# Order of the two kinds of scores within each half of a score phase

## Chip, cores and metric

The kernel runs on one core of one Trainium2 chip. The metric is the device time of one execution in microseconds (us); the time given is the median of several runs. TensorE (PE) does the matmuls; its weight loads are shown as an engine of their own (PEld). VectorE (DVE), ScalarE (ACT) and GpSimd (POOL) work beside it, and each engine takes its instructions in the order in which the program lists them.

## What is computed

A block of two layers over x (4 batches of 512 tokens, 256 features). Each layer is a gated cross attention with 16 heads of 16 features over a context, followed by a gated feed-forward part: in layer 0 with weights quantised to -1, 0 and 1, in layer 1 with one of four experts for each token. Attention is the part that matters here (layer 0; layer 1 has no bias in the softmax, and a relu on q, k and v):

```python
scores = jnp.einsum('bhqd,bhkd->bhqk', Q, K) / math.sqrt(D_K)
time_bias = -0.1 * jnp.abs(t[None, :] - t[:, None])
attn = jax.nn.softmax(scores + time_bias[None, None], axis=-1)
out = jnp.einsum('bhqk,bhkd->bhqd', attn, V)
```

## The kernel before

**Two kinds of scores.** Heads are worked on in 32 groups of four (`groups`, L396: 2 layers x 4 batches x 4), and a head of a group lives in 32 of the 128 partitions. The scores of a group are made twice. First *for the maxima*: `maxima` (L505) multiplies q by k for one tile of 128 queries and two heads into two PSUM tiles `pm`, and VectorE reduces each to its row maximum (L517, `m<-pm`). Once all four query tiles have their maxima, `turned` (L568) transposes them on TensorE (`pmT`, L576) and VectorE subtracts them from q (L578), which gives a shifted query `q2`. Then *shifted*: `weights` (L521) multiplies k by `q2` for one tile of 128 keys and two heads into two PSUM tiles `psc`, and ScalarE takes the exponential of each (L532, `p<-psc`); in layer 0 GpSimd multiplies the block on the diagonal by a decay (L535). Each of these matmuls uses 32 rows of TensorE's array (the program gives pair 0 the first two of the four row groups and pair 1 the last two). `weighted` (L553) multiplies the exponentials of a whole group by the values (`po`, L560).

**Units and score phases.** There are 128 units (32 groups x 4 tiles), and `scores(u, vs)` (L540) is the score phase of unit u: its shifted scores, and, six units ahead, the maxima of unit u + 6. It has two halves. The first holds pair 0 of the maxima and pair 1 of the shifted scores, the second pair 1 of the maxima and pair 0 of the shifted scores. In each half all four matmuls are listed first, and the two functions' drains (two reductions, two exponentials) after them. So a unit fills eight PSUM tiles, in the order pm pm psc psc, pm pm psc psc. Before unit 0 there are only maxima, and in the last six units only shifted scores; units 0 and 1 have two units' maxima each.

**PSUM places.** Every product of TensorE goes to a tile of one pool, `ps` (L55): eight tiles under one tag, each a whole bank. They are given out in turn, so each new tile takes the place of the one eight tiles before it, and its first matmul waits until that one has been read for the last time: by VectorE's reduction if it was a `pm`, by ScalarE's exponential if it was a `psc`, by whatever reads it otherwise.

**Slots.** Behind the score phase of a unit `slot(u)` (L977) lists other work: every fourth unit `weighted`; two units later `turned`, which also transposes and divides the group before (`pn`, L583); and, up to a planned cost of about 3.1 us, steps of chains written out with costs and due times: key and query projections (`pk`, `pq`, L460), values (`pva`, L429), transposes of normalised rows (`pt`, L380), layer 0's feed-forward (`ph`, L640; `py_f`, L388), the output projection (`py_wo`, L388), routing (`plT`, `plg`, `prk`). A slot takes one to four PSUM tiles, which VectorE and ScalarE read. A step of the chains that costs TensorE nothing is the normalisation of a batch's rows: four ACTIVATE instructions on ScalarE (L365, `xn<-x,off,rstd`).

**Stages.** About 40 us of loads and first projections, the units from about 40 to 705 us, and then the experts of layer 1, with gathers and scatters by indirect DMA.

Of the kernel before, what the change touches and what calls it, by code (L numbers as in the profile page):

```python
# [44 lines left out]
def flamingo_kernel(ctx: ExitStack, tc: tile.TileContext, t: dict, out: bass.AP):  # L45
# [494 lines left out]
    def scores(u, vs):  # L540

        ms = [(maxima, v, pair) for v in vs for pair in range(2)]
        ws = [(weights, u, 1 - pair) for pair in range(2)] if 0 <= u < n_units else []
        while ms or ws:
            if ms and ws:
                quad = [ms.pop(0), ws.pop(0)]
            else:
                left = ms or ws
                quad = [left.pop(0), left.pop(0)]
            for drain in [f(w, pair) for f, w, pair in quad]:  # L550
                drain()
# [478 lines left out]
    for u in range(-NT, n_units):  # L1030
        if u == -NT + 1:
            key_rows(0, 1, nc.vector)
            other_half()
            early_none()
            early()
        if u == -NT + 2:
            totals1()
            early_rows()
            totals2()
        if u == 0:  # L1040
            turned(0, None)
            other_constants()
        if u == 4:
            maxima_places(1)
        if u == first_unit(0, B - 1) + 1:
            attn_w.append(load_attn(1))
        if u == first_unit(1, 2) + 2:

            wo1 = [const.tile([P, NF // 2, D], F32, tag=f"cT{i}", name=f"wo1{i}") for i in range(2)]
            for i, w in enumerate(wo1):  # L1050
                rw = t["wo1"][i * FF // 2 : (i + 1) * FF // 2, :]
                nc.sync.dma_start(out=w, in_=rw.rearrange("(c p) f -> p c f", p=P))
        if u == n_units - 1:
            turn_tile(0)
        vs = [u + NT] if u < 0 else [2 * u + NT, 2 * u + NT + 1] if u < LEAD - NT else [u + LEAD]
        scores(u, [v for v in vs if v < n_units])
        slot(u)
# [179 lines left out]
```

## Time and profile before

| what | value |
|---|---|
| median of 3 runs (lowest to highest) | 873.18 us (870.64 to 873.26) |
| the profiled execution's own time | 873.53 us |
| span of the profiled execution | 871.8 us |
| mean granted clock of TensorE | 0.982 |
| TensorE busy from 40 to 700 us | 651.75 of 660 us |
| VectorE, ScalarE busy from 40 to 700 us | 440.8 and 348.9 us |
| reductions `m<-pm` (L517) | 512, mean 682 ns |
| exponentials `p<-psc` (L532) | 512, mean 602 ns |
| score matmuls (L503) | 1024 records for `pm`, 1024 for `psc` |

A row of the timeline gives the start in us from the span's start, the length (of the whole group when instructions are merged), engine, line, operation, the tiles as out<-in, the shapes, and how many (x4); in brackets the time the engine sat idle before it and what ended that. TensorE works a 32-bit matmul off in two passes, so each stands as two records. Matmul ends are modelled, so starts are the surer numbers.

### The profile page before, as it was taken

The numbers are of one execution on the slowest core, as the hardware profiler recorded it, in microseconds if no ns is written. First come the engines' busy times: TensorE is split into PE (matmuls) and PEld (weight loads), VectorE is DVE, ScalarE is ACT, GpSimd is POOL, SyncE is SP. The second block draws the span as 40 slices with busy tenths as digits, with TensorE's granted clock in tenths as the row PEclk, the third lists the DMA queues.
The fourth block names the chain that finished last, engine by engine and source line by source line (L and its number), as shares of the span: only waits on it lengthen the run. The fifth ranks groups of instructions, "written<-read, shape, count | busy, mean of one in ns | idle before, by whom it ended". The sixth has DMA issues, their size and how long they took to land. (4 is left out here: it accounts for less than half of the span.)

```text
span 871.8 us, 13667 instructions
## 1 busy us (share of the span) xinstructions
PE 840.1 (96%) x5290; PEld 476.7 (55%) x5290; DVE 539.9 (62%) x1167; ACT 427.7 (49%) x902; POOL 270.0 (31%) x430
## 2 busy tenths in 40 slices
PE   6899999999999999999999999999999999999995
PEld 3444444445464455545446444554444458999994
DVE  6677878556746675567663776567677715644443
ACT  2765555553645563546543664346565463233331
POOL 5336456324233343312100220012002034445542
PEclk9899999999999999999999999999998899999998
DMA  9100000000001000000000010001001046556650
GB/s 316 55 1 1 1 1 1 1 1 1 2 6 32 1 1 1 1 25 1 1 1 1 25 49 1 1 1 49 2 1 48 2 146 211 155 184 200 198 191 15
DMA packets 17776, 42.03 MB, mean 48 GB/s; under 512 B 2158, under 2 KB 12144, under 8 KB 15280
## 3 DMA queue, kind: packets, MB, share of 16 engines
q0 software_dynamic: 5168, 27.08, 9.5%
q1 hardware_dynamic: 12128, 13.54, 4.6%
q8 instruction: 42, 0.69, 0.3%
q10 hardware_dynamic: 416, 0.54, 0.2%
q14 instruction: 22, 0.18, 0.1%
HBM read 34.86 MB, written 6.68 MB: 48 GB/s over the span
## 5 line engine op out<-in xcount | busy, mean ns | idle before, releaser
L517 DVE TENSOR_REDUCE m<-pm 128x1 f32<-128x512 f32 x512 | 316.9, 682 | 136.3 <-PE psc L503 128.1
L532 ACT ACTIVATE p<-psc 128x512 f32<-128x512 f32 x512 | 267.4, 602 | 161.5 <-PE psc L503 157.2
L503 PE MATMUL psc<-q,k 32*128 32x512 f32 x1024 | 286.4, 636 | 2.1 <-DVE m L517 1.9
L503 PE MATMUL pm<-k,q 32*128 32x512 f32 x1024 | 269.6, 625 | 2.9 <-DVE m L517 2.0
L535 POOL TENSOR_TENSOR p<-p,dec 128x256 f32<-128x256 f32 x128 | 93.5, 734 | 184.0 <-ACT p L532 184.0
L503 PEld LDWEIGHTS pm<-k,q 32*128 32x128 f32 x1024 | 96.7, 186 | 87.6 <-issue 59.9
L503 PEld LDWEIGHTS psc<-q,k 32*128 32x128 f32 x1024 | 108.5, 186 | 55.2 <-issue 26.2
L560 PE MATMUL po<-p,v 128*32 128x512 f32 x1024 | 119.8, 609 | 1.7 <-DVE m L517 1.6
L1075 ACT ACTIVATE ha<-pg,wg 128x128 f32<-128x128 f32 x152 | 43.2, 368 | 88.7 <-PE pg L1069 88.7
L560 PEld LDWEIGHTS po<-p,v 128*32 128x32 f32 x1024 | 32.1, 112 | 85.6 <-issue 64.5
L1069 PE MATMUL pg<-xs,wg 128*128 128x128 f32 x608 | 71.3, 276 | 1.0 <-DVE xn_f L369 1.0
L1069 PEld LDWEIGHTS pg<-xs,wg 128*128 128x128 f32 x608 | 70.4, 192 | 3.0 <-POOL rstd_f L347 1.3
L1085 PE MATMUL pyf<-wo,ha 128*128 128x256 f32 x304 | 68.6, 380 | 0.0
L599 POOL TENSOR_TENSOR x<-x,o 128x256 f32<-128x256 f32 x14 | 10.2, 729 | 174.6 <-DVE o L592 142.7
L640 PE MATMUL ph<-xTf,w1q 128*128 128x512 f32 x128 | 60.2, 603 | 0.0
L1085 PEld LDWEIGHTS pyf<-wo,ha 128*128 128x128 f32 x304 | 56.4, 190 | 6.8
L566 ACT COPY oT<-po 128x512 f32<-128x512 f32 x32 | 18.7, 585 | 84.4 <-PE po L560 84.4
L388 PE MATMUL py_f<-w2q,h 128*128 128x256 f32 x256 | 57.0, 381 | 0.0
L388 PEld LDWEIGHTS py_f<-w2q,h 128*128 128x128 f32 x256 | 48.1, 190 | 9.2 <-DVE m L517 3.0
L1089 DVE TENSOR_TENSOR y<-y,pyf 128x256 f32<-128x256 f32 x19 | 8.0, 421 | 53.3 <-PE pyf L1085 53.0
L460 PE MATMUL pk<-cT,wk 128*128 128x512 f32 x64 | 33.0, 641 | 7.4 <-DMA cT<-in_ctxT_dram 7.3
L640 PEld LDWEIGHTS ph<-xTf,w1q 128*128 128x128 f32 x128 | 22.4, 190 | 27.7 <-issue 17.2
(203 smaller groups left out, 801.6 us busy)
## 6 DMA issues: line engine op xcount, KB each, us to landing
x<-in_x_dram SPq DMA_DIRECT2D x4, 512.0 KB, 8.7
rows_d<-xn_f SPq DMA_DIRECT2D x4, 512.0 KB, 3.7
rows_d<-x SPq DMA_DIRECT2D x4, 512.0 KB, 3.9
cT<-in_ctxT_dram SPq DMA_DIRECT2D x3, 512.0 KB, 9.5
w1q<-in_w_dram SPq DMA_DIRECT2D x1, 1024.0 KB, 9.4
w2q<-in_w_dram SPq DMA_DIRECT2D x1, 1024.0 KB, 11.6
wo<-in_wo_dram SPq DMA_DIRECT2D x2, 512.0 KB, 3.7
rows<-in_rows_dram SPq DMA_DIRECT2D x1, 640.0 KB, 9.6
```

Source lines behind the costliest of these rows:

```text
L388: nc.tensor.matmul(py[:, n, :], lhsT=operand(c, n0 + n), rhs=w[:, c, :], start=(c == 0), stop=(c == chunks - 1),)
L460: nc.tensor.matmul(pp, lhsT=attn_w[layer][w][:, c, ts(tt, P)], rhs=src[:, c, :], start=(c == 0), stop=(c == NC - 1),)
L503: nc.tensor.matmul(out_, lhsT=lhs[r, ts(n, P)], rhs=rhs[r, :], start=True, stop=True)
L517: nc.vector.tensor_reduce(m[:, n, 2 * pair + i, r : r + 1], pm[i], AX.X, ALU.max)
L532: nc.scalar.activation(p[:, i, :], psc[i], AF.Exp, scale=SCALE)
L535: nc.gpsimd.tensor_tensor(d, d, dec.unsqueeze(1).to_broadcast([P, 2, P]), ALU.mult)
L560: nc.tensor.matmul(po[i * HP : (i + 1) * HP, :], lhsT=v_sb[b % 2][0][:, kt, c0 : c0 + HP], rhs=ps_exp[NT * s + kt, i // 2][:, i % 2, :], s ...
L566: nc.scalar.copy(pos[s], po)
L640: nc.tensor.matmul(ph, lhsT=w1q[:, c, ts(f, P)], rhs=st["xT"][:, c, :], start=(c == 0), stop=(c == NC - 1),)
L1069: nc.tensor.matmul(ph[:, f, :], lhsT=w[:, c, ts(f2 * NF // 2 + f, P)], rhs=xs[j][:, c, :], start=(c == 0), stop=(c == NC - 1),)
L1075: nc.scalar.activation(ha[:, f, :], ph[:, f, :], AF.Gelu, bias=wg[j][:, NC * FF + fa : NC * FF + fa + 1],)
L1085: nc.tensor.matmul(py, lhsT=hs[j, f // 4][:, f % 4, :], rhs=wo1[f // 4][:, f % 4, :], start=(f == 0), stop=(f == NF - 1),)
```

## The change

In `scores`, where a half has both kinds, the shifted scores are taken first and the maxima second. A unit's eight PSUM tiles then come in the order psc psc pm pm, psc psc pm pm. The pairs that meet in a half stay the same; so do the halves that hold only one kind. In each half the exponentials are now listed ahead of the reductions, which stand on another engine.

```diff
@@ -543,7 +543,7 @@
         ws = [(weights, u, 1 - pair) for pair in range(2)] if 0 <= u < n_units else []
         while ms or ws:
             if ms and ws:
-                quad = [ms.pop(0), ws.pop(0)]
+                quad = [ws.pop(0), ms.pop(0)]
             else:
                 left = ms or ws
                 quad = [left.pop(0), left.pop(0)]
```

## Prediction

> **What bounds the kernel now.** First the page's busy shares and the row of TensorE in 40 slices.
>
> ```profile
> PE 840.1 (96%) x5290; PEld 476.7 (55%) x5290; DVE 539.9 (62%) x1167; ACT 427.7 (49%) x902; POOL 270.0 (31%) x430
> PE   6899999999999999999999999999999999999995
> ```
>
> TensorE is full from about 40 to 700 us, where the 128 score phases ("units") lie; a unit and the slot work behind it take some 5 us. Whatever makes TensorE wait there is time. So I read one undisturbed unit in the timeline, engine by engine. It starts at 288.28; the first fence is TensorE, the second the first instruction of each draining engine and the first weight load of the slot work behind the unit.
>
> ```profile
> 288.28 0.70 PE L503 MATMUL pm<-k,q 32*128 32x512 f32 x2
> 288.29 0.70 PE L503 MATMUL psc<-q,k 32*128 32x512 f32 x2
> ...
> 289.67 0.59 PE L503 MATMUL psc<-q,k 32*128 32x512 f32 x2
> 289.68 0.59 PE L503 MATMUL pm<-k,q 32*128 32x512 f32 x2
> 290.20 3.70 PE L640 MATMUL ph<-xTf,w1q 128*128 128x512 f32 x8
> ```
> ```profile
> 289.44 0.69 DVE L517 TENSOR_REDUCE m<-pm 128x1 f32<-128x512 f32 x1 [3.08 <-PE psc L503]
> 289.58 0.60 ACT L532 ACTIVATE p<-psc 128x512 f32<-128x512 f32 x1 [0.59 <-PE psc L503]
> 290.20 0.19 PEld L640 LDWEIGHTS ph<-xTf,w1q 128*128 128x128 f32 x1 [0.76 <-DVE m L517]
> ```
>
> The four matmuls of a half start within 0.02 us: they run side by side in four row groups, so their order in the half is worth 0.01 us by itself. The unit's last matmul starts at 289.68 and slot work follows 0.52 us later, 1.93 us after the unit began. I find that 0.52 in every undisturbed unit: TensorE's own pace. The row names a reduce as what ended the loader's wait, and rightly: the slot's first PSUM place is the unit's first place (eight places, used in turn), and its reduce ended at 289.44 + 0.69 = 290.13, only 0.07 before. It costs nothing today, but has next to no slack.
>
> **What the change does.** In the built program each mixed half now issues psc, psc, pm, pm; nothing is added or removed, and VectorE, ScalarE and GpSimd keep their own order, as do SP's queue and all DMAs. What changes is who frees a place eight places on. A slot's first two places wait for the unit's first two exps instead of its first two reduces, the third and fourth for reduces instead of exps. After a slot of two places, the next unit's places 3 and 4 wait for exps 3 and 4 instead of reduces 3 and 4, and reduces 3 and 4 are wanted half a phase later.
>
> **Part 1, clean units: +0.6 us.** First exp: 289.58 + 0.60 = 290.18, 0.05 behind the first reduce, and two places earlier in the half it ends 0.01 sooner. A matmul that a drain releases starts 0.05 behind its end in the trace (many score matmuls do), so the slot starts at about +1.94 for +1.93: 0.01 x some 30 units = 0.3. Slots that open with `po` in layer 0 wait for two semaphores and follow 0.11 behind; nine of these x 0.04 = 0.3.
>
> [...]
>
> **Part 2, units whose exps are late: the main term.** ScalarE is a queue in order, and the four normalisation rows of L365 (28 + 28 instructions, 14 groups of four) stand ahead of a unit's exps. At 402.47:
>
> ```profile
> 403.09 2.07 ACT L365 ACTIVATE xn_a<-x,off_a,rstd_a 128x256 f32<-128x256 f32 x4
> 405.06 2.03 ACT L532 ACTIVATE p<-psc 128x512 f32<-128x512 f32 x4
> ```
> ```profile
> 404.40 0.19 PEld L388 LDWEIGHTS py_wo<-wo,oTT 128*128 128x128 f32 x1 [0.76 <-DVE m L517]
> ```
>
> The exps wait until 405.06; the first ends at 405.64 (two take 1.06, one 0.58). Today nobody cares: the slot opens at 404.40 on the place that a reduce freed. Afterwards it opens at 405.64 + 0.05 = 405.69, and TensorE stands for 1.29 us. I looked at every group of L365 inside the score stage: 13 units (starts 128.09, 155.24, 220.68, 255.90, 309.83, 361.58, 402.47, 476.47: 1.27 to 1.30 us each; 497.33, 590.41, 667.39: 1.23; 507.29, 599.37: 0.55, where the slot is late already). Gross: 8 x 1.28 + 3 x 1.23 + 2 x 0.55 = 15.0.
>
> Some comes back, because the next unit already waits for something that the late exps or the slot's drains cause, and that does not move as much. Unit 159.51, behind 155.24, runs 1.17 over the clean 1.93: about 1.1 back. 481.19, behind 476.47, runs 0.40 over: 0.4 back. Behind 590.41 and 667.39 the next unit is held today by the late exps (0.84 over); reckoned place by place it ends 0.28 later instead of 1.23: 1.9 back for both. At 497.33 the slot is a transpose of those same rows, whose second half runs at +2.91 today and could at +3.72: 0.8 paid, 0.4 back. The others are followed by units with 0 to 0.07 over, or by a drain chain that moves along: nothing back. Net: 15.0 - 3.9 = **+11.1**.
>
> **Part 3, slots that a late reduce holds today: -2.4.** At 102.50 VectorE has a quantising step between reduces:
>
> ```profile
> 106.06 1.16 DVE L295 SCALAR_TENSOR_TENSOR w1q<-w1q,qthr_w,neg_w 128x512 f32<-128x512 f32 x1
> 107.14 0.68 DVE L517 TENSOR_REDUCE m<-pm 128x1 f32<-128x512 f32 x1
> ```
> ```profile
> 107.96 1.50 PE L560 MATMUL po<-p,v 128*32 128x512 f32 x12 [0.64 <-DVE m L517]
> ```
>
> That idle 0.64 goes, since the exps are long done. The same kind of gap: 0.49 at 89.69, 0.52 at 586.84, 0.47 at 120.81, 0.21 at 139.80 and 0.11 at 680.42 (last score matmul + 0.52 against the slot's start). What is late next there is VectorE's own backlog: in the stretches 78 to 110 and 113 to 126 it has hardly a gap, so I count only the place where such a stretch ends and leave out two more (0.7 each) inside one.
>
> **Part 4, reduces wanted half a phase later: -1.4.** Units behind a two-place slot stop waiting at place 4 for reduce 4: 0.26 at 375.67, 0.4 at 121.83, 0.15 at 677.71, 0.6 at 689.97. Others are held by the last places of the unit, which wait for the slot's own drains; these keep their place (1.39 instead of 0.97 into the unit, some 15 units) and stay. Bounds: 0, if exp 4 is as late, to 4.5, the sum of today's waits at place 4.
>
> **Part 5, turned slots: -1.0.** `pn` behind `pmT` starts at +2.50, 0.05 behind reduce 2; exp 2 ends 0.06 sooner: 0.07 x 10 + 0.04 x 6.
>
> **Sum.** 0.6 + 11.1 - 2.4 - 1.4 - 1.0 = **+6.9 us**. The profiled execution took 873.5 us (span 871.8); the median of the runs is 873.2, so the difference is the same against either: **880.4 us**.
>
> **Rivals.**
> 1. *Faster.* Reduces, not exps, are the slow drain: VectorE is 62% busy against 49%, and the waits view has more than ten lines in which a matmul or load waits for the reduce. If the late exps are handed back by later waits everywhere, as behind 155.24 (part 2 falls to 2), and parts 3 to 5 reach their upper bounds (2.4 + 1.4, 4.5, 1.0), the sum is 0.6 + 2 - 9.3 = -6.7: 867 us. It decides once more than about three quarters of the 15.0 comes back. Against it: by the rows of part 2, eight of the 13 units hand nothing back.
> 2. *No change.* Part 2 at about 5 (some six of its 11.1 handed back as well, by more successors like 159.51): 0.6 + 5 - 4.8 = +0.8: 874 us.
> 3. *More.* Nothing is handed back and VectorE's backlog eats parts 3 and 4: 0.6 + 15.0 - 1.0 = +14.6: 888 us.
> That the program keeps its order is excluded by its listing.
>
> **How the numbers follow.** Forecast 0.70 (876 to 885), rival 1 0.08, rival 2 0.13, rival 3 0.09. A run can tell 0.3% (2.6 us) from no change, so slower 0.79, same 0.13, faster 0.08. The range reaches over rival 2's centre and most of rival 3: 874 to 887.
>
> **What would show it.** Right: in the 13 units the slot's first load is released by the exp (ACT p L532), TensorE stands about 1.2 us there, and the waits view gets 10 to 15 us of TensorE or its loader behind ACT p; DVE's lines for `po`, `pk`, `ph` and `pmT` shrink; the gap at about 107.9 is gone; clean units still take 1.93 to 1.95. Wrong: clean units grow by more than 0.05 (part 1 mis-sized, 100 units), or no unit waits for an exp, or the rows of L365 come at another time than before.

## The result, and the profile after

| | before | changed | changed / before |
|---|---|---|---|
| median of the runs compared (lowest to highest) | 873.12 us (870.64 to 873.26, 4 runs) | 885.89 us (885.43 to 886.52, 4 runs) | 1.0155, 95% interval 1.0143 to 1.0166 |
| span of the profiled execution | 871.8 us | 884.4 us | |
| mean granted clock there | 0.982 | 0.982 | |

Slower by 12.8 us where 7.2 was forecast (880.4: the sum of 6.9 on top of the profiled 873.5). First the page of the changed kernel: busy shares, TensorE's slices, and the row of the granted clock.

```profile
PE 842.2 (95%) x5290; PEld 481.5 (54%) x5290; DVE 539.2 (61%) x1167; ACT 426.3 (48%) x902; POOL 270.6 (31%) x430
PE   6899999999999999999999999999999999999995
PEclk9999999999999999999999999999998789999998
```

The same work in a longer span. Only the clock row has something to ask about: ahead of the last slices it has an 8, a 7 and an 8, where the kernel before has two eights.

The clean unit that started at 288.28 now starts at 289.67; timeline of the changed kernel, its first and last score matmul, its drains, and the first weight load of its slot:

```profile
289.67 0.70 PE L503 MATMUL psc<-q,k 32*128 32x512 f32 x2
...
290.89 1.57 ACT L532 ACTIVATE p<-psc 128x512 f32<-128x512 f32 x3 [0.51 <-PE pm L503]
290.91 1.89 DVE L517 TENSOR_REDUCE m<-pm 128x1 f32<-128x512 f32 x3 [3.05 <-PE pm L503]
...
291.60 0.30 PEld L640 LDWEIGHTS ph<-xTf,w1q 128*128 128x128 f32 x2 [0.76 <-ACT p L532]
```

The slot follows 1.93 us after the unit's start, as before, but the loader's releaser is now the exponential. The exponentials also start earlier: 1.22 into the unit, where it was 1.30.

The unit that started at 402.47 now starts at 406.27 (timeline, ScalarE, VectorE and the loader):

```profile
406.89 2.07 ACT L365 ACTIVATE xn_a<-x,off_a,rstd_a 128x256 f32<-128x256 f32 x4
...
407.51 2.48 DVE L517 TENSOR_REDUCE m<-pm 128x1 f32<-128x512 f32 x4 [3.05 <-PE pm L503]
...
408.86 1.54 ACT L532 ACTIVATE p<-psc 128x512 f32<-128x512 f32 x3
409.49 0.51 PEld L388 LDWEIGHTS py_wo<-wo,oTT 128*128 128x128 f32 x3 [2.06 <-ACT p L532]
```

The slot opens 3.22 us into the unit instead of 1.93. The first reduction is over at about 408.2, but nobody waits for it; the first exponential, behind the four rows of L365, ends 0.05 before the load. In the waits view (total, times, longest, in us) of the changed kernel:

```profile
PEld pmT L576 <- ACT p L532: 20.2, 25, 2.0
PEld pk L460 <- ACT p L532: 10.6, 13, 2.1
PEld py_wo L388 <- ACT p L532: 8.2, 4, 2.1
PE py_wo L388 <- ACT p L532: 4.9, 4, 1.2
```

The loader's rows are not loss as they stand: a clean unit has 0.76 in them. What the longest (2.1) have beyond that, and TensorE's own row (four times 1.2 at `py_wo`), is.

**Where the time went, unit by unit.** I took the start of each score phase and of the slot behind it in both traces and noted where the changed kernel's lag grows or shrinks (places are starts in the kernel before):

| place | part of the prediction | predicted | measured |
|---|---|---|---|
| clean units, 1.93 in both | 1 | +0.6 | 0.0 |
| the 13 units with late exps: eight by 1.27 to 1.30, three by 1.23 or 1.24, two by 0.55 | 2, gross | +15.0 | +15.1 |
| units behind five of them (159.51, 481.19, 502.49, 593.85, 670.84) | 2, handed back | -3.9 | -3.2 |
| slots that a late reduce held (77.28, 102.50, 117.57, 137.63, 580.74, 677.71; nothing at 83.84, whose slot is the 89.69 of the prediction) | 3 | -2.4 | -2.5 |
| place 4 (121.83, 375.67, 684.54) | 4 | -1.4 | -1.1 |
| 15 slots, 13 of them turned, 0.10 to 0.16 each | 5 | -1.0 | -1.8 |
| 204.26, 298.64, 412.01, 528.23: 0.22 each | none | 0 | +0.9 |
| 324.97, 367.14, 417.72, 451.25, 544.89, 623.78, 635.55: 0.08 to 0.24 | none | 0 | +1.2 |
| first units, 31 to 42 (clock) | none | 0 | -0.8 |
| the rest, singly up to 0.5, both signs | none | 0 | +0.4 |
| **lag where the units with maxima end (694)** | | **+6.9** | **+8.2** |
| end of the score stage, 694 to 709 | none | 0 | +3.8 |
| behind it | none | 0 | +0.6 |
| **span** | | **+6.9** | **+12.6** |

Up to 694 us the sum holds within 1.3. Beyond it comes a term that the prediction does not have. The windows view at that place (span of the window, busy us of each engine, and behind POOL the mean granted clock, the DMA share and GB/s), the kernel before, then the changed one:

```profile
693.00:700.00 7.00, 7.00 (x48) 4.74 (x46) 3.76 (x14) 2.34 (x5) 0.73 (x1) 0.74 0.01 2
700.00:707.00 7.00, 7.00 (x52) 2.06 (x48) 0.04 (x1) 2.86 (x6) 5.40 (x6) 0.76 0.63 197
707.00:714.00 7.00, 6.96 (x49) 4.87 (x42) 1.25 (x4) 6.98 (x13) 1.60 (x2) 1.00 0.66 258
```
```profile
700.00:707.00 7.00, 7.00 (x28) 4.42 (x28) 4.63 (x12) 2.66 (x5) 0.73 (x1) 0.50 0.01 2
707.00:714.00 7.00, 7.00 (x34) 3.96 (x38) 0.75 (x5) 1.95 (x4) 2.72 (x3) 0.50 0.13 42
714.00:721.00 7.00, 6.80 (x49) 2.62 (x42) 0.88 (x4) 2.99 (x7) 3.55 (x4) 0.90 0.90 334
```

By the clock records the changed kernel runs at half clock from 698.4 to 715.5 (17.1 us), the kernel before from 689.7 to 696.6 and from 700.0 to 703.4 (10.2). TensorE is all but full there (6.80 to 7.00 of 7 us in the rows above) and the clock is 0.50, so by an estimate from these two about half of the 6.9 us more is lost, 3.4 of the 3.8. The largest piece is the small matmuls of L860, 24 records that took 2.87 us at full clock before and 5.29 at half clock now (timeline, the kernel before and the changed one):

```profile
696.49 2.87 PE L860 MATMUL pid_d<-tid_d,sel_d 128*128 128x9 f32 x24
```
```profile
704.66 5.29 PE L860 MATMUL pid_d<-tid_d,sel_d 128*128 128x9 f32 x24
```

### The profile page after: what moved, and what is told of

It reads as the page before. It is cut to its first block, busy times and chain, and to the rows that moved or that the text cites. A ratio compares the mean times of both kernels' runs of the same rounds, so it can differ in the third digit from the quotient of the medians.

```text
span 884.4 us, 13653 instructions
## 1 busy us (share of the span) xinstructions
PE 842.2 (95%) x5290; PEld 481.5 (54%) x5290; DVE 539.2 (61%) x1167; ACT 426.3 (48%) x902; POOL 270.6 (31%) x430
## 4 chain that ended last, share of the span: by engine, by line
PE 76%; issue 6%; ACT 5%; DVE 4%; DMA 4%; POOL 4%; POOLq 0%; ACTq 0%; DVEq 0%
PE psc L503 15%; PE pm L503 14%; PE po L560 13%; PE py_f L388 6%; PE ph L640 6%; PE pk L460 4%; PE pva L429 3%; PE pq L460 3%; DMA out_dram<-y,put 2%; PE pmT L576 2%; PE py_wo L388 2%; PE pg L1069 2%; DVE m L517 2%; PE pn L583 1%; ACT xn_f L365 1%
## 5 line engine op out<-in xcount | busy, mean ns | idle before, releaser
L532 ACT ACTIVATE p<-psc 128x512 f32<-128x512 f32 x512 | 264.5, 603 | 155.4 <-PE pm L503 137.3
L503 PE MATMUL pm<-k,q 32*128 32x512 f32 x1024 | 286.1, 628 | 1.6 <-ACT q L492 0.9
L503 PE MATMUL psc<-q,k 32*128 32x512 f32 x1024 | 269.4, 627 | 2.4 <-DVE m L517 1.5
L503 PEld LDWEIGHTS pm<-k,q 32*128 32x128 f32 x1024 | 111.5, 185 | 57.2 <-issue 25.7
L503 PEld LDWEIGHTS psc<-q,k 32*128 32x128 f32 x1024 | 95.1, 187 | 83.3 <-issue 48.8
L599 POOL TENSOR_TENSOR x<-x,o 128x256 f32<-128x256 f32 x14 | 10.2, 731 | 179.9 <-DVE o L592 146.7
## 6 DMA issues: line engine op xcount, KB each, us to landing
w2q<-in_w_dram SPq DMA_DIRECT2D x1, 1024.0 KB, 11.5
```

The lines of the kernel that those rows point to most:

```text
L503: nc.tensor.matmul(out_, lhsT=lhs[r, ts(n, P)], rhs=rhs[r, :], start=True, stop=True)
L532: nc.scalar.activation(p[:, i, :], psc[i], AF.Exp, scale=SCALE)
```

## Experiments

No kernel here leaves out or changes any of the computation; they only order it differently. Where an edit is one condition, it stands in the line that the change touches:

```diff
-                quad = [ws.pop(0), ms.pop(0)]
+                quad = [ws.pop(0), ms.pop(0)] if COND else [ms.pop(0), ws.pop(0)]
```

**The 13 units left in the old order** (COND: `u not in (21, 26, 37, 43, 53, 61, 69, 81, 85, 87, 101, 103, 117)`).

> The swapped order everywhere but in the 13 units whose first exponential stands behind the normalisation rows (units 21, 26, 37, 43, 53, 61, 69, 81, 85, 87, 101, 103, 117); those keep the order of before. Theory A (those 13 slots carry the loss): up to the last mixed unit the kernel is 3 to 4 us ahead of before; with the last 15 us of the score stage at half clock as in the changed kernel (+3.8) it ends at 873 to 874 us, without that at 869 to 870. Rival B (the loss is spread over all slots, a little each): only a tenth of it goes, 884 us.

Measured 866.75 us (865.93 to 871.0, 7 runs) against 872.93 of the kernel before: ratio 0.9949, 0.9931 to 0.9967. The loss is gone and a gain is left, larger than theory A said. At the old 402.47, timeline of this kernel, ScalarE and the loader:

```profile
400.10 2.07 ACT L365 ACTIVATE xn_a<-x,off_a,rstd_a 128x256 f32<-128x256 f32 x4
...
401.41 0.94 PEld L388 LDWEIGHTS py_wo<-wo,oTT 128*128 128x128 f32 x5 [0.76 <-DVE m L517]
...
402.08 0.58 ACT L532 ACTIVATE p<-psc 128x512 f32<-128x512 f32 x1
```

The slot opens 0.67 us ahead of the exponential, on a reduction's place. Up to 653 us the lag is -3.0, of which -0.5 came about in the first units, where the clock differs; at 708 it is -7.8. Between 650 and 720 us this trace has 6.8 us of half clock and the kernel before 17.1, so most of the surprise is clock (below).

**The new order in those 13 units alone** (COND: `u in` the same list).

> The order of before, swapped in those 13 units alone. Theory A: the lag up to the last mixed unit is about +12 us, and the end of the score stage keeps the clock of before: 884 to 886 us. Rival B: 874 to 875 us. Rival C (the longer half clock at the end follows from any shift of the stage, not from the order of the last mixed unit): 888 to 889 us.

Measured 883.62 us (882.96 to 884.48, 4 runs), ratio 1.0132, 1.0117 to 1.0146: 0.4 under theory A's range and far from the rivals. Its lag at 653 us is +11.8, where theory A said about +12; the two rows of part 2 in the table above come to 11.5 up to there.

**The new order everywhere but in unit 121, and in unit 121 alone** (COND: `u != 121`; `u == 121`). Unit 121 is the last one with both kinds of scores; it starts at 684.54, just ahead of the half clock.

> The swapped order everywhere but in unit 121, the last one that has maxima. Theory A (with the half clock at the end set off by that unit's order): 3.8 us of the end come back and 0.6 of that unit is lost: 882 to 883 us. Rival C: the long half clock stays, 886 to 887 us.

> The order of before, swapped in unit 121 alone. Theory A: 0.6 us gained in that unit, then 17 us at half clock instead of 10: 876 us. Rival C: the clock of before, 872.5 us.

Measured 883.31 us (882.64 to 883.8, 4 runs; 1.0123, 1.0108 to 1.0137) and 869.29 us (868.08 to 876.1, 12 runs; 0.9973, 0.9957 to 0.9989). My theory that the order in unit 121 sets off the longer half clock falls both ways: kept, the 17.1 us of half clock stay (from 696.9); alone, the kernel gets faster. The first time is near theory A's 882 to 883, but not by its cause: this trace has no half clock between 659 and 675, where the kernel before and the changed one have 6.8 us each. The second lies below both forecasts, and holds a lesson. Up to unit 121 its order is that of the kernel before, and still this is the windows view at 659 us, the kernel before and then this one:

```profile
652.00:659.00 7.00, 5.97 (x39) 3.20 (x35) 6.72 (x16) 4.21 (x8) 0.00 (x0) 1.00 0.00 0
659.00:666.00 7.00, 7.00 (x33) 2.09 (x33) 4.09 (x10) 2.28 (x4) 2.44 (x8) 0.51 0.00 0
```
```profile
652.00:659.00 7.00, 5.97 (x36) 3.36 (x37) 6.69 (x18) 4.15 (x8) 0.00 (x0) 1.00 0.00 0
659.00:666.00 7.00, 6.48 (x57) 2.04 (x50) 3.97 (x9) 3.28 (x8) 2.44 (x8) 1.00 0.00 0
```

The same work, the same stand of TensorE ahead of it (1.03 us in both), once followed by 6.8 us of half clock and once not: 2.4 us of lag that the order cannot have made. Its 12 runs spread over 8 us, and the longer ones have the lower clock: 866.4 us of span at a mean clock of 0.989, 871.0 at 0.982, 874.4 at 0.978.

**The new order in the first half of each unit alone, and in the second half alone** (COND: `len(ws) == 2`; `len(ws) == 1`).

> The new order in the first half of a unit alone; the second half as before. The slot behind a unit opens on the places of the first half. Theory A (the loss is the slot's first two places waiting for exps that stand behind the rows of L365): the whole loss of the 13 units stays, some +11.5 to +12 in the score stage, the gains at slots that a late reduce held stay too, the gain at place 4 (1.4) is lost: 884 to 888 us. Theory B (what counts is which drain holds the last places of a unit): nothing of the loss is left, 870 to 875.

> The new order in the second half of a unit alone. The slot's first two places are freed by reduces again. Theory A: no unit waits for a late exp at its slot, the 13 units lose nothing; place 4 waits for an exp instead of a reduce (-1.4, less where exps are late, as behind the 13 units): 870 to 874 us. Theory B: most of the loss stays, 880 or more.

Measured 882.65 us (878.66 to 883.88, 4 runs; 1.0105, 1.0086 to 1.0125) and 873.28 us (871.5 to 874.75, 12 runs; 0.9995, 0.9985 to 1.0005). The loss sits in the first half, whose places the slot takes: all 13 stands are there at 1.23 to 1.30 or 0.55, and the median is 1.3 under theory A's range. The two longer runs (883.88) have a mean clock like that of the kernel before (0.983), the two shorter ones a higher one (0.987 and 0.991). The second half by itself is worth nothing that can be told: it gains 0.26 at 375.67 and 0.58 at 684.54 and gives 0.38 back at 593.85 and at 670.84, behind late exps.

**The rows out of the way of the exps.** The step `norm` (L365) is kept back until the next unit's scores are listed, and the transposes that need its rows come one unit later (in all three chains that have them; one is shown); once with the new order, once with the old:

```diff
-            [(stats, 0, 0), (more_stats, 0, 1), (norm, 0, 1), (turn, 0.9, 1)],
+            [(stats, 0, 0), (more_stats, 0, 1), (norm, 0, 1), (turn, 0.9, 2)],
...
-            job()
+            pending.append(job) if job.__name__ == "norm" else job()
...
         scores(u, [v for v in vs if v < n_units])
+        while pending:
+            pending.pop(0)()
```

> The changed kernel with the four normalisation rows of L365 issued behind the next unit's scores, so that ScalarE has the unit's exps ahead of the rows; the transposes that need the rows come one unit later. To be read against the next kernel, which has the same rows with the order of the kernel before. Theory A (the loss comes from exps behind the rows): with no late exp left only the gains remain, so this kernel is 3 to 7 us faster than the next one. Theory B (a place freed by an exp is worse by itself, wherever the rows stand): it is 8 to 12 us slower than the next one.

> The kernel before with the rows of L365 issued behind the next unit's scores, as in the kernel ahead. Both theories: within 4 us of the kernel before (869 to 877), since there the slots open on reduces; it is the measure for the kernel ahead.

Measured 869.89 us with the new order (867.95 to 872.31, 8 runs) and 876.92 with the old (875.98 to 879.15, 6 runs): 7.0 us faster, at the upper end of theory A. The move by itself costs: with the old order it is 3.6 us slower than the kernel before (1.0054, 1.0037 to 1.007), with the new one 3.4 faster (0.9969, 0.9953 to 0.9986). Between the two, the same change that costs 12.8 us gains 7.0 once the exps stand ahead of the rows; by the traces the lag between the two is 0.0 at 42 us and -6.6 at 652, so this is not clock. Timeline of the first of the two at the old 402.47:

```profile
400.74 2.06 ACT L532 ACTIVATE p<-psc 128x512 f32<-128x512 f32 x4 [0.43 <-PE pm L503]
...
401.51 3.10 PEld L388 LDWEIGHTS py_wo<-wo,oTT 128*128 128x128 f32 x15 [0.76 <-ACT p L532]
...
402.66 2.08 ACT L365 ACTIVATE xn_a<-x,off_a,rstd_a 128x256 f32<-128x256 f32 x4
```

The slot still opens on an exponential's place, 1.93 us into the unit.

**The idle stretch ahead of the half clock.** In unit 121 TensorE waits for reductions that stand behind 17 small steps of the token lists (L773 to L827) on VectorE. First these steps were moved behind the reductions, in the changed kernel and in the one that keeps the 13 units:

```diff
-            job()
+            if u == 120 and job.__name__ in ("lists", "token_places", "by_tile"):
+                pending.append(job)
+            else:
+                job()
```

> The changed kernel with the 17 small VectorE steps of the token lists (L773 to L827 of the changed kernel) moved from ahead of the reduces of unit 121 to behind them; nothing else. The changed kernel's TensorE idles for 1.46 us in that unit, waiting for a reduce behind these steps, and the 17.1 us of half clock begin in the next clock window. Theory A (the idle stretch sets off the half clock): no half clock between 690 and 720, about 17.1 x 0.44 = 7.5 less and 1.5 less for the idle stretch, up to 2.5 back for the later lists: 876 to 880 us, mean clock 0.988 or more. Theory B (the half clock comes by itself, or from the small matmuls of L860): 10 us or more of half clock stay near 700, 884 to 887 us.

> The new order in all units but the 13 with late exps, and the small VectorE steps behind the reduces of unit 121. Theory A (both costs are apart from one another): the 866.7 of the 13 kept units, less 6.8 x 0.44 = 3 of half clock and up to 1.5 of idle, plus up to 2.5: 862 to 866 us. Theory B (the half clock stays): 866 to 869.

Measured 882.85 us (882.28 to 883.86, 4 runs; 1.0101, 1.0084 to 1.0118) and 866.41 us (866.1 to 870.29, 6 runs; 0.9928, 0.991 to 0.9947). The first lies between the ranges, with 10.2 us of half clock from 703.2, which is what theory B said of the clock; the second lies in theory B's range, 0.3 us below the kernel without the move. But the edit did not do what theory A needs: the stand was not taken away; it moved, and the half clock with it. So the matmuls of L860 were moved as well, one slot later, behind `po`:

```diff
+                if u == 123 and "gathered" in c["steps"][0][0][0].__qualname__:
+                    continue
```

> The changed kernel with the 17 small VectorE steps behind the reduces of unit 121 and the matmuls of L860, which wait for them, one slot later, behind unit 124 and its weighted values: TensorE has other work in both places where it idled. Theory A (the half clock at the end of the score stage follows an idle stretch of TensorE): no half clock between 690 and 725, 17.1 us x 0.4 = 7 less, and 1.5 of idle: 876 to 879 us. Theory B (the half clock comes by itself or from the matmuls of L860): 10 us or more of half clock stay there, 882 to 886 us.

> The same two moves on the kernel that keeps the old order in the 13 units with late exps. Theory A: no half clock near 690 either, 6.8 x 0.4 = 2.7 and up to 1.5 of idle less than 866.5: 861.5 to 864 us. Theory B: 866 to 868 us.

Measured 887.35 us (884.36 to 888.09, 5 runs; 1.0165, 1.0145 to 1.0186) and 872.66 us (870.62 to 875.52, 12 runs; 1.0003, 0.999 to 1.0016): worse, and above the ranges of both theories, since now unit 124 waits for the shift of its query (L578), which VectorE has behind the same steps, and later TensorE waits 1.97 and 2.42 us for the gathers. TensorE's stand ahead of the half clock, in the changed kernel, with the steps moved, and with the matmuls moved too (timeline rows of three kernels):

```profile
698.74 2.07 PE L503 MATMUL psc<-q,k 32*128 32x512 f32 x2 [1.46 <-DVE m L517]
```
```profile
702.87 1.37 PE L860 MATMUL pid_d<-tid_d,sel_d 128*128 128x9 f32 x7 [2.61 <-DVE sel_d L848]
```
```profile
704.12 1.24 PE L503 MATMUL psc<-q,k 32*128 32x512 f32 x4 [4.41 <-DVE q L578]
```

The half clock begins at 698.4, 703.2 and 702.5 in these three: within the stand in the first and the third, 0.3 us behind it in the second. It goes where the stand goes, which speaks against theory B (that it comes by itself at a fixed place or from L860: in the third kernel it comes ahead of L860). That it goes away without a stand was not shown, because none of the edits removed the stand. Nor does every half clock have a long stand ahead of it: the 6.8 us that begin at 667.7 in the changed kernel follow a window with only 0.27 us.

**What is left.** Two kernels are the fastest: the new order without the 13 units (866.75), and the same with the list steps moved (866.41). Their intervals (0.9931 to 0.9967 and 0.991 to 0.9947) overlap, so the list steps earn nothing that can be told; the plain one is 19 us under the changed kernel.

## Why the prediction was right, and where it was not

- **The size: near, and in part by luck.** 885.89 lies 0.9 above the 876 to 885 to which the forecast gave 0.70, and within the wider 874 to 887. Up to 694 us the sum is only 1.3 short, because what was missed on one side (2.1 in eleven units, 0.8 in part 2) meets what was missed on the other (0.6 in part 1, 0.8 in part 5, 0.8 in the first units).
- **Direction and mechanism: right, and shown.** The slot now waits for exps that stand behind the rows of L365: the new order in 13 units alone gives +11.8 us in the trace, leaving it out there gives a gain, and taking the rows out of ScalarE's way turns a loss of 12.8 into a gain of 7.0.
- **Part 2: sized right.** Gross 15.1 against 15.0; handed back 3.2 against 3.9, since the unit at 159.51 gave back 0.7 and not 1.1, and the two behind 590.41 and 667.39 gave 1.7 and not 1.9 (the prediction's items add up to 3.8; it took off 3.9). Net 11.9 for 11.1.
- **Part 1: no cost at all** (0.6 predicted). The exps start 0.08 earlier in the new order, not 0.01, so the place that an exp frees is ready when TensorE's own pace gets there. My 0.01 came from the start times of the four matmuls in a half; why the exps gain 0.08 was not tested.
- **Parts 3 and 4: their gains are right** within 0.3 together, part 3 in part by luck: the 0.49 counted at 89.69 did not come, and 0.54 came at 77.28, where none had been counted.
- **Part 5: under-sized**, 1.8 for 1.0.
- **The step of part 4 that failed is "these keep their place (1.39 instead of 0.97 into the unit, some 15 units) and stay".** Eleven units paid 2.1 that the sum had at nothing. In four the last place waits for VectorE's drain of the slot, which does not come earlier when the unit does: seen from the unit's start it ends 0.2 later. In seven the premise of the prediction itself is wrong: places are not always given in turn. By a count in the built program, which no trace here shows, 37 of some 1350 tiles before and 70 after take another place than that of the tile eight before. In these seven units the last score tile gets the place of the unit's own first one, now freed by the unit's own first exp: in the trace that exp releases the load of the last score matmul, 1.81 to 1.87 into the unit. At 367.14 (before) and 371.12 (changed), the load of the last score matmul:

```profile
368.77 0.29 PEld L503 LDWEIGHTS psc<-q,k 32*128 32x128 f32 x2 [0.46 <-DVE q L496]
```
```profile
372.34 2.07 ACT L532 ACTIVATE p<-psc 128x512 f32<-128x512 f32 x4 [0.42 <-PE pm L503]
...
372.99 0.29 PEld L503 LDWEIGHTS pm<-k,q 32*128 32x128 f32 x2 [0.70 <-ACT p L532]
```

  1.63 into the unit before, 1.87 after, for a drain of the slot there and for its own first exp here.
- **The missing term: the clock, +3.8 at the end of the score stage and -0.8 at its start** (there 3.4 us of half clock from 32.8, where the kernel before has 6.8 from 31.0). The prediction took the clock row of the page as given. How much of it belongs to the change stays open. For it: all four runs of the changed kernel have 32 to 39 us of half clock (span x 2 x (1 - mean clock)), 54 runs of the kernel before 23 to 35 with a median of 30; some 5 us more half clock are by an estimate about 2 us of time (from the 0.46 to 0.49 us for each in the last section). Against it: the 13 units alone make no more of it than before (23 to 25), nor does the new order without them (19 to 31), and the same order can come with and without it (659 us above). Whether the cost depends on how a stand falls on the grid of the clock's records was not shown: no run here tests it, and which half clock a change will meet was not predictable from the page.
- **Rivals.** The first two needed some 13 and 10 of the 15.0 handed back, and 3.2 was. The third came near in time (888), but for another reason than it gave: 3.2 was handed back, and parts 3 and 4 were not eaten.

## What to carry to other kernels

Before swapping who frees a buffer, look at each new freeing engine's queue for what stands ahead of the freeing instruction, not at the mean length of the two drains: the clean units showed nothing and 13 made most of the result. If the bad cases are few and known in advance, keep the old order there; or move the foreign work behind the drain, which made the same change a gain, though the move had a cost of its own. And a sum over stages should name the stands of TensorE that may cost the clock: here, up to 850 us, those of 1.46 us or more within 3.41 us were followed by half clock in 25 of 25 windows (below).

## What the runs showed of the hardware

In the traces the granted clock changes on a grid and is 1.0 or 0.5. Its records begin on multiples of 3.41 us from the first one's start, and all but the last end there: those of the changed kernel are 20.5, 3.4, 631.5, 6.8, 23.9, 17.1 and 163.8 us long ahead of the last. Over the 14 traces of this case these are the windows of 3.41 us on that grid at full clock that end ahead of 850 us, by how long TensorE stood still in them, and the clock of the next window:

| stood still within one window of 3.41 us | windows | next one at half clock |
|---|---|---|
| 1.46 us or more | 25 | 25 |
| 1.0 to 1.32 us | 61 | 8 |
| 0.3 to 0.96 us | 185 | 2 |
| less than 0.3 us | 3082 | 10 |

So in these traces the stands of 1.23 us in the 13 units were never followed by half clock when they were alone in a window, and 1.46 us or more within a window always was. That is no rule, though. Behind 850 us, 5 of 19 windows with 1.46 us or more (1.58 to 1.95) were followed by full clock. And the last row has half clock without a long stand: four times behind a window with 0.27 us, six times behind one with none, which itself followed a half-clock window. How long the half clock then lasts (3.4, 6.8, 10.2 or 17.1 us) did not follow the length of the stand, and what decides it is open. What it costs can be read at the stretch of scores and slots that starts at 653.87 in the kernel before: in the new order it took 10.53 us in the three traces with no half clock there, and 13.66 to 13.87 in the four with 6.8 us of it, which is 0.46 to 0.49 us for each; the 0.44 and 0.4 in the expectations were estimates.
